# Last mixture of a gated four-layer block: sorted rows in a DRAM region for each expert, and another order of the stages

## The chip, the cores and the metric

The kernel runs on one core of a Trainium2 chip. Its time is the device time of one execution in microseconds (us). Engines are named as in the profile: PE (TensorE) with its weight loads PEld, DVE (VectorE), ACT (ScalarE), POOL (GpSimd) and SP (SyncE, which here only issues DMAs).

## The reference, cut to what matters

The input x holds 16 batches of 256 rows of 128 numbers. Four layers follow each other; each adds a gated cross attention (16 heads of 8 over 64 context rows) and then a gated feed-forward part:

```python
x = x + tanh(g_xattn[0]) * L0_xattn(layernorm(x), ctx, ctx)     # stage 0
x = x + tanh(g_ffn[0])   * L0_ffn(layernorm(x))                 # stage 1: mixture, best 2 of 8 experts, and a shared one
x = x + tanh(g_xattn[1]) * L1_xattn(layernorm(x), ctx, ctx, mask, side)  # stage 2
x = x + tanh(g_ffn[1])   * L1_ffn(layernorm(x))                 # stage 3: one ternary matrix
x = x + tanh(g_xattn[2]) * L2_xattn(...)                        # stage 4
x = x + tanh(g_ffn[2])   * L2_ffn(layernorm(x))                 # stage 5: one expert
x = x + tanh(g_xattn[3]) * L3_xattn(...)                        # stage 6
x = x + tanh(g_ffn[3])   * L3_ffn(layernorm(x))                 # stage 7: mixture, best 1 of 8 experts

def L3_ffn(t):                     # the part that is changed
    prob = softmax(t @ switch_w + switch_b)
    gate, e = max(prob), argmax(prob)          # first largest
    return gate * (gelu(t @ w1[e] + b1[e]) @ w2[e] + b2[e])      # 128 -> 512 -> 128
```

All is float32.

## The kernel before, in words

**Halves and blocks.** The batches are cut into two halves of 8 (hf 0 and 1). A half has 2048 rows, 16 row tiles of 128, and 4 blocks of 512 rows (two batches). x stays in SBUF (`xs`) through all layers. The halves depend on each other only through engines and buffers, so a stage of one half can run beside any stage of the other.

**The order is made by a planner in the kernel.** Each piece of work is a Python generator (`attention` for one batch, `queries`, `ffn_ternary`, `ffn_expert1`, `block`, `sorted_pair` and so on) that yields requests: `op(engine, length, needs)`, `dma(queue, size, needs)` or `get(slots, number, needs)`. `Order.run` (L173 to L201) takes the request that can begin first by its own assumed lengths, and of equal ones (rounded to 0.1 us) the one of the smallest rank; then the generator issues its instructions. So the program's order on PE, DVE, ACT and SP is that in which the planner took the requests, and POOL is chained to the same order (`chain_gpsimd`, L216). On the chip each engine runs its own instructions in that order and waits on semaphores; the planner's times play no part there. `RANKS` (L87) gives the rank of each of the 8 stages of each half, and `RATE` (L82) the assumed bytes per us of a DMA.

**A mixture (`mixture`, L1296, for l = 0 and l = 3).** For each block, `block` computes the layernorm, transposes it (`turned`), multiplies by the gate matrix (L1374) and puts the logits for 4 row tiles into a common tile `rt` (L1392). The normalized rows go to DRAM (`xrow`, L1345), and for l = 3 the rows of x beside them (L1351). When all four blocks of the half are done (`normed`), one chain on DVE does the routing for all 16 row tiles at once: softmax (L1410 to L1417), first largest (L1421 to L1428), counts by two matmuls (L1458, L1459), running sums (L1464), regions of the experts rounded up to 128 rows (L1471 to L1475), and then the inverse of the permutation: one-hot matrices (L1528, L1537, L1544) and 16 matmuls (L1549) give for each of n sorted rows the number of the row that belongs there. n = 16 k + 7 tiles: 39 for l = 0 (k = 2) and 23 for l = 3 (k = 1). The result is `index` (where a sorted row comes from), `place` (where its result goes) and, for l = 3, `gates`; `ex` holds the expert of each tile.

**The sorted tiles.** `fetch` (L1634) loads for each tile its expert's weights, 578 KB, by SP: the expert's number is read into a register (`value_load`, L1643), then the DMA is issued (L1647). There are 6 buffers `wb`. `sorted_pair` (L1652) works on two tiles: POOL gathers the rows by an indirect DMA (L1671, buffers `xg`), PE transposes them (L1684), DVE copies (L1688), PE does four matmuls a tile for the first matrix (L1698), ACT the gelu (L1705), PE four for the second (L1717), DVE adds the bias (L1727, after which `wb` is free) and, for l = 3, multiplies by the gate and adds x (L1734, after which `xg` is free); then POOL scatters the rows to the output (L1753). Between two indirect DMAs that would stand next to each other POOL gets a small addition (`apart`, L440). In float32 each matmul shows as two records. For l = 0 the results go to DRAM (`ysort`) and are gathered again (`collect`).

**Other lines that are named below.** Layernorm: L644, L645 (DVE), L647 to L650 (POOL), L656 (ACT). Attention ends with the projection L781 and the addition to x, L787. `make_fill1` loads the side input of layer 1's attention for one batch (four DMAs of 64 KB, three buffers) on SP, and POOL prepares it (L972).

Of the kernel before, what the change touches and what calls it, by code (L numbers as in the profile page):

```python
# [36 lines left out]
F32 = mybir.dt.float32  # L38
# [33 lines left out]


# [8 lines left out]
REACH, LAND, RATE, SWAP = 0.1, 1.8, 250e3, 1.3  # L82
# [4 lines left out]
RANKS = ((11, 14, 2, 14, 3, 5, 4, 14), (14, 14, 4, 14, 6, 9, 6, 2))  # L87
# [150 lines left out]
def flamingo_kernel(  # L238
# [91 lines left out]
    for l, k in ((0, 2), (3, 1)):  # L330
        n = sorted_tiles(k)
        for hf in range(2):
            wide = D if l == 0 else 2 * D
            xd = dram.tile([NT * P, wide], F32, name=f"xrow{l}{hf}", tag=f"xrow{l}{hf}")
            yd = None
            if l == 0:
                yd = dram.tile([n * P, D], F32, name=f"ysort{l}{hf}", tag=f"ysort{l}{hf}")
            srt[l, hf] = (k, n, xd, yd)
# [43 lines left out]
    starts = cst([1, nmax], "starts")  # L382

    id32 = cst([P, 32], "id32")
    ksel = cst([P, 2, 2, 2, 32], "ksel")
# [13 lines left out]
    label = cst([P, NT, 5], "label", BF16)  # L399
# [23 lines left out]
    big_s = slots("big", [P, 2, 512], 4)  # L423
    rc0_s = slots("rc0", [P, P], 3)
    wb_s = slots("wb", [P, NPK], 6)
    xg_s = slots("xg", [P, 2 * D], 6)
    xgT_s = slots("xgT", [P, 2 * P], 2)
    y_s = slots("y", [P, 2, D], 3)
# [6 lines left out]
    expert_s = slots("expert", [1, nmax], 2, I32)  # L435
# [53 lines left out]
    def constants():  # L489
# [31 lines left out]
        nc.vector.tensor_copy(label[:, :, 0:2], lab)  # L521
# [10 lines left out]
        nc.gpsimd.memset(carry[:, :, 0:1], 0.0)  # L532
        yield op(POOL, 0.5)
# [21 lines left out]
        nc.gpsimd.memset(ksel, 0.0)  # L555
        yield op(DVE, 0.5)
        for h in range(2):
            nc.vector.tensor_copy(
                ksel[:, h, :, h, :], id32.unsqueeze(1).to_broadcast([P, 2, 32])
            )  # L560
        yield op(DVE, 0.5)
        nc.vector.tensor_copy(id32b, id32)
        nc.vector.tensor_copy(kselb, ksel)
# [257 lines left out]
    def unit0(pair, t, rank):  # L821
# [57 lines left out]
        else:  # L879
            (sb,) = yield get(big_s, 1)  # L880
            sm = sb.ap.rearrange("p a b -> p (a b)")
# [108 lines left out]
    def attention(l, b, rank, end):  # L990
# [7 lines left out]
        i32, ks = (id32, ksel) if fb else (id32b, kselb)  # L998
# [226 lines left out]

    def add_four(blk, py, end, event, at):
# [30 lines left out]
    def ffn_expert1(blk, rank, begin, end):  # L1257

        (xn,) = yield get(xn_s, 1, begin[2 * blk], begin[2 * blk + 1])
        ats = yield from layernorm(blk, begin, xn.ap, xn)  # L1260
        (xf,) = yield get(xf_s, 1)
# [5 lines left out]
        (hb,) = yield get(big_s, 1)  # L1267
        h = hb.ap
# [24 lines left out]
    def bc8(a):  # L1293
        return a.unsqueeze(2).to_broadcast([P, NT, E])

    def mixture(l, hf, rank, begin, end):  # L1296

        k, n, xd, yd = srt[l, hf]
        b0 = HB * hf
        blks = range(NBLK // 2 * hf, NBLK // 2 * (hf + 1))  # L1300
        xnt = None
        if l == 0:
            (xnt,) = yield get(xnT_all_s, 1, begin[b0], moe_ready)
# [5 lines left out]

        index = st.ap[:, 4 * NT : 4 * NT + n].bitcast(I32)  # L1310
        place = st.ap[:, NT : NT + n].bitcast(I32)
        gates = st.ap[:, NT + n : NT + 2 * n]
# [17 lines left out]
        kept = Event(len(blks) * (1 if l == 0 else 3))  # L1330
# [18 lines left out]
        def keep_x(b):  # L1349
            at = yield dma(SP, 131e3, begin[b])  # L1350
            nc.sync.dma_start(rows(2 * (b - b0), 2)[:, :, D:], xs[b])  # L1351
            order.set(kept, at)

        def block(blk):
# [5 lines left out]
            if l == 3:  # L1360
                for b in (2 * blk, 2 * blk + 1):
                    order.task(rank, keep_x(b))
            xf = None
            if l == 0:
                dst, need = xnt.ap[:, blk - blks[0], :], xnt
            else:
                (xf,) = yield get(xf_s, 1)
                dst, need = xf.ap, xf
            pe, at = yield from turned(xn.ap, dst, ats, need)
# [3 lines left out]
            for t in range(4):  # L1373
# [3 lines left out]
                    gw0 if l == 0 else gw3,  # L1377
# [3 lines left out]
            if xf:  # L1381
                give(xf, xf_s, at)
            else:
                order.set(ev[blk], at)
# [3 lines left out]
            if l == 0:  # L1388
                nc.vector.tensor_copy(mine_, pl3)
            else:  # L1390
                swb = rows_sb[:, R_SWB : R_SWB + E]
                nc.vector.tensor_tensor(  # L1392
                    mine_, pl3, swb.unsqueeze(1).to_broadcast([P, 4, E]), ALU.add
                )
# [5 lines left out]
        if l == 0:  # L1400
            shared_left, routed = [len(blks)], Event()
            for blk in blks:
                order.task(rank + 0.6, shared_expert(blk, xnt, ev[blk], routed, end, rank, shared_left))
# [15 lines left out]
        def first_largest(p, m, oh):  # L1419

            nc.vector.tensor_reduce(m, p, AX.X, ALU.max)  # L1421
            nc.vector.tensor_tensor(oh, p, bc8(m), ALU.is_equal)

            nc.vector.scalar_tensor_tensor(
                oh, oh, 2.0 * E, falling.unsqueeze(1).to_broadcast([P, NT, E]), ALU.mult, ALU.add
            )
            nc.vector.tensor_reduce(c1, oh, AX.X, ALU.max)
            nc.vector.tensor_tensor(oh, oh, bc8(c1), ALU.is_equal)  # L1428

        yield op(DVE, 1.6)  # L1430
        first_largest(p3, m1, te(oh1))
        if k == 2:
            yield op(DVE, 1.9)
            nc.vector.scalar_tensor_tensor(te(p2), te(oh1), -2.0, p3, ALU.mult, ALU.add)
            first_largest(te(p2), m2, te(oh2))
            yield op(DVE, 0.6)
            nc.vector.tensor_tensor(den, m1, m2, ALU.add)
            nc.vector.reciprocal(den, den)
            for m in (m1, m2):
                nc.vector.tensor_tensor(m, m, den, ALU.mult)  # L1440
# [483 lines left out]
```

## Time and profile before

| | us |
|---|---|
| median of 3 runs | 1087.75 |
| lowest and highest | 1085.69, 1087.98 |
| the profiled execution | 1091.78 |
| its span in the profile | 1090.0 |

| engine | busy us | share of the span |
|---|---|---|
| PE | 914.4 | 84% |
| DVE | 670.9 | 62% |
| POOL | 644.8 | 59% |
| ACT | 575.9 | 53% |

The profile names groups of instructions by line, engine, operation and tiles (out<-in), with count, busy time, mean length, and the idle time of the engine before them with what ended it. The view by stretches gives for each stretch its length, the busy time of PE, PEld, DVE, ACT and POOL with the number of records, the granted clock of PE (1.00 is full), the share of time in which the DMA engines are busy, and GB/s. The timeline gives start, length, engine, line and operation. The weights are the largest traffic: 124 loads of 578.0 KB, of 114.36 MB in all. Half 1's last mixture is the end of the program: the last gate matmul (L1374) begins at 970.27 us, the routing's last DVE operation ends at 995.50, the last matmul (L1717) at 1083.26.

### The profile page before, as it was taken

Reading aid. Unit: us, or ns where it says so; the run is one execution under the profiler, and the core shown is the slowest. Engines: PE = TensorE matmul, PEld = TensorE weight load, DVE = VectorE, ACT = ScalarE, POOL = GpSimd, SP = SyncE. Lnnn points to the kernel's source line nnn. Section 1 sums busy time; section 2 is a strip of 40 time slices with the busy share of each in tenths; the row PEclk is TensorE's granted clock in tenths of the full one; section 3 lists DMA queues with packets and bytes.
Section 4 is the critical chain, followed back from the end, with each engine's and each line's share of the span. In section 5 each row is a group of like instructions: output and inputs, shape, how many; then the busy total and the mean of one; then the engine's idle time right before and its main releaser. Section 6 shows DMA issues by size and latency. Waiting matters only on the chain.

```text
span 1090.0 us, 27621 instructions
## 1 busy us (share of the span) xinstructions
PE 914.4 (84%) x10480; PEld 724.2 (66%) x10480; DVE 670.9 (62%) x1832; ACT 575.9 (53%) x1345; POOL 644.8 (59%) x1055
## 2 busy tenths in 40 slices
PE   5887568989788987789789899999998999777765
PEld 3776346878686886677556667667665667666664
DVE  4798897754464224366776767879789645446221
ACT  5454243656443454566446557765765667553332
POOL 5787636666834654765557656533444666744675
PEclk9899788979889998899999999999999999987987
DMA  6000004467764774633100100100000425544672
GB/s 195 2 12 21 23 1 147 132 211 237 231 153 162 227 228 141 228 93 112 52 17 20 29 16 21 36 21 7 24 9 2 161 59 156 189 145 144 215 259 60
DMA packets 63477, 114.36 MB, mean 105 GB/s; under 512 B 10289, under 2 KB 42552, under 8 KB 63344
## 3 DMA queue, kind: packets, MB, share of 16 engines
q1 hardware_dynamic: 54688, 94.22, 26.8%
q0 software_dynamic: 8224, 17.45, 6.0%
q8 instruction: 82, 1.34, 0.5%
q10 hardware_dynamic: 432, 0.93, 0.3%
q14 instruction: 51, 0.42, 0.1%
HBM read 99.06 MB, written 14.42 MB: 104 GB/s over the span
## 4 chain that ended last, share of the span: by engine, by line
PE 38%; DVE 12%; issue 8%; DMA 6%; POOL 5%; ACT 3%; another core or an unknown queue 2%; SPq 0%; POOLq 0%; DVEq 0%; ACTq 0%
PE bank L1698 6%; PE bank L1717 6%; DMA xg<-xrow,state 4%; DVE mx L1093 3%; PE bank L1008 3%; PE bank L1175 3%; PE bank L1072 2%; PE bank L781 2%; PE bank L1134 2%; PE bank L1014 2%; PE bank L747 1%; PE bank L1197 1%; PE bank L669 1%; PE bank L1621 1%
## 5 line engine op out<-in xcount | busy, mean ns | idle before, releaser
L1705 ACT ACTIVATE big<-bank,wb 128x128 f32<-128x128 f32 x496 | 138.5, 382 | 156.2 <-issue 98.6
L1698 PE MATMUL bank<-xgT,wb 128*128 128x128 f32 x992 | 147.5, 301 | 21.9 <-DVE xgT L1688 14.0
L1671 POOL DMA_INDIRECT xg<-xrow,state x124 | 121.9, 983 | 63.5 <-issue 27.9
L1698 PEld LDWEIGHTS bank<-xgT,wb 128*128 128x128 f32 x992 | 134.1, 212 | 31.7 <-DVE xgT L1688 18.6
L1717 PE MATMUL bank<-wb,big 128*128 128x128 f32 x992 | 133.6, 287 | 5.8 <-issue 4.8
L1717 PEld LDWEIGHTS bank<-wb,big 128*128 128x128 f32 x992 | 126.2, 200 | 13.8 <-issue 10.9
L656 ACT ACTIVATE xn<-x,ln 128x128 f32<-128x128 f32 x256 | 107.6, 494 | 52.5 <-POOL ln L650 52.2
L1727 DVE TENSOR_TENSOR y<-bank,wb 128x128 f32<-128x128 f32 x124 | 32.3, 285 | 115.4 <-PE bank L1717 90.9
L894 POOL TENSOR_TENSOR pT<-pT,rc 128x1024 f32<-128x1024 f32 x32 | 75.2, 2366 | 45.2 <-DVE rc L889 12.3
L1779 POOL DMA_INDIRECT yg<-ysort,state x64 | 62.9, 983 | 56.5 <-DVE x L1787 26.3
L1093 DVE TENSOR_REDUCE mx<-bank 128x8 f32<-128x512 f32 x128 | 81.4, 682 | 20.9 <-PE bank L1014 6.3
L1162 ACT ACTIVATE pT<-bank 128x512 f32<-128x512 f32 x128 | 67.2, 601 | 36.3 <-PE bank L1149 30.2
L677 POOL TENSOR_TENSOR x<-x,rows_sb 128x256 f32<-128x256 f32 x96 | 71.3, 761 | 12.5 <-ACT xn L656 11.8
L644 DVE BATCH_NORM_STATS2 ln<-x 128x6 f32<-128x128 f32 x256 | 68.6, 268 | 2.4 <-DMA x<-in_x_dram 2.2
L648 POOL TENSOR_TENSOR ln<-ln,mhalf 128x4 f32<-128x4 f32 x64 | 66.7, 1043 | 5.3
L1008 PE MATMUL bank<-kexp,qT 32*128 32x256 f32 x768 | 69.4, 413 | 0.2 <-DVE mx L1093 0.2
L647 POOL TENSOR_SCALAR ln<-ln 128x4 f32<-128x4 f32 x64 | 14.7, 230 | 90.9 <-DVE ln L645 83.7
L1753 POOL DMA_INDIRECT out_dram<-y,state x46 | 47.1, 1023 | 27.6 <-DVE y L1727 20.6
L1046 DVE TENSOR_REDUCE mx<-bank 128x8 f32<-128x512 f32 x64 | 43.5, 682 | 29.8 <-PE bank L1014 14.2
L1175 PE MATMUL bank<-pT,vx 128*32 128x256 f32 x768 | 60.3, 399 | 0.8 <-DVE pT L1054 0.5
L1688 DVE COPY xgT<-bank 128x256 f32<-128x256 f32 x64 | 25.9, 409 | 55.1 <-PE bank L1684 37.9
L1684 PE MATMUL bank<-ident,xg 128*128 128x128 f32 x124 | 29.4, 306 | 34.2 <-DMA xg<-xrow,state 30.1
(230 smaller groups left out, 2094.2 us busy)
## 6 DMA issues: line engine op xcount, KB each, us to landing
wb<-in_pk_l_dram SPq DMA_DIRECT2D x124, 578.0 KB
ysort<-y SPq DMA_DIRECT2D x38, 128.0 KB
xrow<-xn SPq DMA_DIRECT2D x16, 256.0 KB
fill<-in_fsideT_dram SPq DMA_DIRECT2D x64, 64.0 KB
x<-in_x_dram SPq DMA_DIRECT2D x16, 128.0 KB
xrow<-x SPq DMA_DIRECT2D x16, 128.0 KB
xg<-xrow,state POOLq DMA_INDIRECT x124
yg<-ysort,state POOLq DMA_INDIRECT x64
```

What stands on the lines that cost most here:

```text
L644: nc.vector.bn_stats(st[:, 2 * i + j, :], xs[b][:, j, :])
L656: nc.scalar.activation(xn[:, k, :], xs[b][:, j, :], AF.Identity, bias=nm[:, k : k + 1], scale=rs[:, k : k + 1],)
L677: nc.gpsimd.tensor_tensor(xs[b], xs[b], row.unsqueeze(1).to_broadcast([P, 2, D]), ALU.add)
L894: nc.gpsimd.tensor_tensor(s3, s3, rc.ap.unsqueeze(1).to_broadcast([P, 8, P]), ALU.mult)
L1008: nc.tensor.matmul(dst(g), qT[strip(g), ts], kexp[strip(g)].rearrange("p h k -> p (h k)"), start=True, stop=False,)
L1093: nc.vector.tensor_reduce(mx[:, :, g, :], sc[g].ap.rearrange("p (t h k) -> p t h k", h=4, k=S2), AX.X, ALU.max,)
L1162: nc.scalar.activation(pTs[g // 2].ap[:, (g % 2) * 512 : (g % 2 + 1) * 512], sc[g].ap, AF.Exp)
L1175: nc.tensor.matmul(po.ap[strip(g), i * S : (i + 1) * S], vx.ap[:, b % 2, c, :], pTs[c // 4].ap[:, (c % 4) * S : (c % 4 + 1) * S], start=Tr ...
L1671: nc.gpsimd.indirect_dma_start(out=xg[i], out_offset=None, in_=xd, in_offset=bass.IndirectOffsetOnAxis(ap=index[:, 2 * q + i : 2 * q + i + ...
L1698: nc.tensor.matmul(ph.ap[:, cs], wb[i].ap[:, cs], xgT.ap[:, i * P : (i + 1) * P], start=True, stop=True,)
L1705: nc.scalar.activation(hb.ap[:, i, cs], ph.ap[:, cs], func, bias=wb[i].ap[:, PK_B1 + c : PK_B1 + c + 1],)
L1717: nc.tensor.matmul(py.ap[:, i * D : (i + 1) * D], hb.ap[:, i, c * P : (c + 1) * P], wb[i].ap[:, PK_W2 + c * D : PK_W2 + (c + 1) * D], star ...
```

## The change

**The last mixture (l = 3) becomes a function of its own, `last_mixture`; the first one keeps the code above (`first_mixture`).** Each half gets a DRAM tensor of 17280 rows of 258 numbers: a region of 2048 rows for each of the 8 experts, and 7 x 128 rows to spare. A row holds the normalized row, the row of x, its number in the output and its gate. Each block does its own routing for 4 row tiles as soon as its logits are there: softmax, first largest, counts by two matmuls over 32 columns. `next_` holds for each expert the next free row of its region and runs on from block to block (a scan over 5 values an expert). POOL then scatters the block's 4 row tiles to their places in the regions (four indirect DMAs of 128 rows). ACT copies x beside the normalized rows in the tile that is scattered.

When all four blocks have counted, a short chain on DVE works out for each of the 23 tiles its expert and its first row in the regions (both to `ex`), and bounds that tell which of its rows are filled. A tile is now 128 rows that follow each other: SP reads the first row's number into a register and loads the tile by a plain DMA; POOL gathers nothing for l = 3. Gate and output row come with the rows; two small DVE operations a tile set the place of an unfilled row out of bounds. The scatter to the output is as before.

**The regions are filled once** with numbers (a piece of `rows_sb`), so that unfilled rows hold something finite: `fill_regions` issues 27 DMAs a half on SP, each of 128 x 5 rows; the planner is told to begin them at given stages.

**The planner** gets other ranks and RATE 280e3 for 250e3. Smaller edits: `ex` is given back by count (`done_with`), `big` is 1032 wide for 1024, `xg` 258 for 256, `y` 258 for 256 (the places are kept in it), the tile `ksel` is gone (it was only copied to `kselb`), `rt` is cut into four pieces after the second mixture of layer 0, and `ffn_expert1` takes its `big` buffer one step earlier.

```diff
-REACH, LAND, RATE, SWAP = 0.1, 1.8, 250e3, 1.3
+REACH, LAND, RATE, SWAP = 0.1, 1.8, 280e3, 1.3
-RANKS = ((11, 14, 2, 14, 3, 5, 4, 14), (14, 14, 4, 14, 6, 9, 6, 2))
+RANKS = ((10, 14, 14, 1, 1, 12, 8, 14), (14, 14, 2, 7, 5, 9, 10, 15))
...
+ROW3 = 2 * D + 2
+REGION = NT * P
+NROWS = E * REGION + (E - 1) * P
...
+    def last_mixture(hf, rank, begin):
...
+        next_ = st.ap[:, 4 * NT : 4 * NT + E]
+        yield op(DVE, 0.1, st)
+        nc.vector.tensor_copy(next_, region)
...
+        def block(blk):
...
+            (xn,) = yield get(big_s, 1, begin[bs[0]], begin[bs[1]])
+            rows = xn.ap.rearrange("p (t c) -> p t c", c=ROW3)
+            ats = yield from layernorm(blk, begin, rows[:, :, 0:D], xn)
...
+            for i, b in enumerate(bs):
+                yield op(ACT, 0.35, begin[b])
+                nc.scalar.copy(rows[:, 2 * i : 2 * i + 2, D : 2 * D], xs[b])
...
+            nc.tensor.matmul(pb.ap[:, 0:32], ones, cnt, start=True, stop=True)
+            nc.tensor.matmul(pb.ap[:, 32:64], before, cnt, start=True, stop=True)
...
+            nc.vector.tensor_tensor_scan(
+                upto, carry4.rearrange("p e t -> p (e t)"), acc, 0.0, ALU.mult, ALU.add
+            )
+            nc.vector.tensor_copy(next_, upto3[:, :, 4])
+            order.set(counted, at)
...
+            for t in range(t0, t0 + 4):
+                at = yield op(POOL, 1.3, placed)
+                part_indirect()
+                ins = nc.gpsimd.indirect_dma_start(
+                    out=xd,
+                    out_offset=bass.IndirectOffsetOnAxis(ap=pos[:, t : t + 1], axis=0),
+                    in_=rows[:, t - t0, :],
+                    in_offset=None,
+                )
+                unordered(ins, f"x{l}{hf}")
+                at = (at[0] + 2.2, "DMA")
+                order.set(kept, at)
...
+    def fill_regions(hf, whens):
+        xd = srt[3, hf][2].rearrange("(p a) c -> p a c", p=P)
+        n, m = NROWS // P, 5
+        for i in range(n // m):
+            yield dma(SP, 4.0 * P * m * ROW3, whens[i * m * len(whens) // n])
+            nc.sync.dma_start(
+                xd[:, m * i : m * (i + 1), :],
+                rows_sb[:, 0:ROW3].unsqueeze(1).to_broadcast([P, m, ROW3]),
+            )
...
         for i in range(m):
+            if l == 3:
+                yield op(SP, 0.4, *xgs, *needs)
+                r = nc.sync.value_load(
+                    ex.ap[0:1, n + 2 * q + i : n + 2 * q + i + 1], min_val=0, max_val=NROWS - P
+                )
+                at = yield dma(SP, 132e3)
+                nc.sync.dma_start(xg[i], xd[bass.ds(r, P), :])
+                done_with(ex, at)
+                continue
             at = yield op(POOL, 1.3, *xgs, *needs)
...
+                nc.vector.scalar_tensor_tensor(
+                    yi[i], yi[i], xg[i][:, 2 * D + 1 :], xg[i][:, D : 2 * D], ALU.mult, ALU.add
+                )
+                nc.vector.tensor_tensor(
+                    place[:, i : i + 1], xg[i][:, 2 * D : 2 * D + 1].bitcast(I32),
+                    filled[:, t : t + 1], ALU.bitwise_and,
+                )
+                nc.vector.tensor_tensor(
+                    place[:, i : i + 1], place[:, i : i + 1], empty[:, t : t + 1], ALU.bitwise_or
+                )
...
+    whens = [X[i][b] for i, h in ((5, 0), (6, 0), (3, 1), (4, 1)) for b in range(HB * h, HB * h + HB)]
+    for hf in range(2):
+        order.task(100.0, fill_regions(hf, whens[16 * hf : 16 * hf + 16]))
```

## The prediction

> **What bounds the kernel now.** I read the page's engine shares first, then TensorE's busy time in chosen stretches, then the groups of the last stretch, then the timeline of one pair of tiles there. The page says that TensorE (PE) leads, and the line by slices that it falls off at the end:
>
> ```profile
> PE 914.4 (84%) x10480; PEld 724.2 (66%) x10480; DVE 670.9 (62%) x1832; ACT 575.9 (53%) x1345; POOL 644.8 (59%) x1055
> PE   5887568989788987789789899999998999777765
> ```
>
> PE works 914 of 1090 us, so what a change of order can win is a part of the 176 us of idle. The stretches were cut where the work changes: 963.2 is the end of the last attention (the last addition on L787, at 963.23), 996 the end of half 1's routing, 1083.3 the last matmul.
>
> ```profile
> 480.00:890.00 410.00, 376.50 (x4693) 271.18 (x4693) 307.87 (x889) 249.63 (x544) 225.79 (x454) 0.98 0.14 40
> 890.00:963.20 73.20, 65.02 (x700) 51.39 (x700) 32.07 (x99) 49.33 (x114) 45.65 (x81) 0.95 0.46 143
> 963.20:996.00 32.80, 20.43 (x143) 18.36 (x141) 22.44 (x82) 11.82 (x33) 15.32 (x27) 0.80 0.45 138
> 996.00:1083.30 87.30, 62.49 (x439) 58.01 (x439) 19.91 (x64) 28.72 (x104) 58.19 (x96) 0.88 0.64 204
> ```
>
> The columns are length, busy PE, weight loads, DVE, ACT, POOL, then granted clock, DMA share and GB/s. The first two rows are idle 8% and 11%; the last two 38% and 28%, at a granted clock of 0.80 and 0.88. What PE waits for in the last one, by groups (busy, mean ns, then idle before and who ended it):
>
> ```profile
> L1698 PE MATMUL bank<-xgT,wb 128*128 128x128 f32 x208 | 32.9, 324 | 12.2 <-DVE xgT L1688 9.1 <-DVE y L1734 1.9 <-issue 1.1
> L1684 PE MATMUL bank<-ident,xg 128*128 128x128 f32 x23 | 6.2, 313 | 13.7 <-DMA xg<-xrow,state 13.7
> L1753 POOL DMA_INDIRECT out_dram<-y,state x25 | 25.4, 1015 | 17.2 <-DVE y L1727 14.5 <-issue 2.7
> L1671 POOL DMA_INDIRECT xg<-xrow,state x23 | 22.7, 986 | 18.5 <-issue 16.0 <-PE bank L1717 1.9 <-PE bank L1698 0.3
> ```
>
> Of the 24.8 us of idle, 13.7 are transposes that wait for gathered rows and 12.2 matmuls that wait for the copy of the transposes (the two overlap by a little). The gathers are late because POOL issues them in order among the scatters: 25 + 23 issues and 48 separators of 0.21 us fill 58 of 87 us. A stretch has 208/8 = 26 tiles, so a tile takes 87.3/26 = 3.36 us here, of which PE works 2.40. A pair whose rows are there looks like this:
>
> ```profile
> 1051.40 0.38 PE L1684 MATMUL bank<-ident,xg 128*128 128x128 f32 x2
> 1052.78 2.05 PE L1698 MATMUL bank<-xgT,wb 128*128 128x128 f32 x16
> 1054.66 2.12 PE L1717 MATMUL bank<-wb,big 128*128 128x128 f32 x16
> ```
>
> That is 0.38 + 2.05 + 2.12 = 4.55 us a pair, 2.28 a tile, and the next pair starts 5.2 us after (1056.62).
>
> **The change, part by part.** Both programs' orders of issue (they hold no times) give the tiles on each side of the last attention.
>
> *Moved: the last tiles.* Before the last attention there stood 15 first matmul groups (L1698), 12 second ones (L1717) and 16 transposes of half 0's tiles; in the changed program 6, 4 and 8. At 1.03, 1.04 and 0.19 us each (half of 2.05, and near half of 2.12 and 0.38) that is 9.3 + 8.3 + 1.5 = 19.1 us of PE work gone from in front of 963.2. With nothing else changed the last attention ends at 963.2 - 19.1 = 944.1.
>
> *Removed: the routing gap.* In 963.2 to 996 PE idles 12.4 us while the routing of all 16 row tiles runs on DVE (106 instructions for both halves, with one of 2.29 us and five of 0.49). It is replaced by a short chain for each block of 4: some 22 DVE operations at 0.16 to 0.30 us, about 5 us, an exponential, two small matmuls and four scatters at 1.02 + 0.36 us on POOL. Only the last block's chain follows the last attention: layernorm to gate took 963.57 to 971.23 (7.7 us), then 5 + 1.6 (table load 1.28 and 0.31) + 5.5 and a landing of up to 5, together 25 us. Behind the last attention stand 17 tiles of half 0 (40 first groups less half 1's 23), 17 x 2.7 = 46 us. So I cost it at nothing; if the tiles were gone it would cost its 25.
>
> *Replaced: the gathers.* 46 gathers leave POOL; 32 scatters of rows come, before the last stretch but for four to eight. POOL per tile falls from 2 x (1.0 + 0.21 + 0.15) = 2.7 us to 1.4. The rows now come by SP: one more register load and DMA for a tile. Weight loads that wait for nothing are issued about 1.17 us apart (the first two of the last stretch at 995.09 and 996.27), so SP takes 2.34 us a tile, just above PE's 2.28. The first row load of a half also waits for all 16 scatters of its half, and behind it stand the weights of the later pairs, as behind every waiting load all later weights and rows; for half 1 the 17 tiles above cover that, 46 us against 25. The ring: when a pair's buffers come free, SP needs 3 x 1.17 = 3.5 us to its fourth load; by the trace's DMA packets a weight load lands 3.2 to 6 us after its issue (the worst here 8.9); transposes, copy, matmuls and gelu to the addition take 6.7 (1046.39 to 1053.73, less some waiting). 3.5 + 5 + 6.7 = 15.2 us for three pairs is 2.5 us a tile, inside the next figure.
>
> *The pace of the last tiles.* Lower bound 2.28 (PE alone), upper bound 3.36 (nothing gained). I take 2.28 plus the wait for the copy, 12.2/26 = 0.47, and no wait for rows: 2.75. It is nearer the clean pair's 2.6. The trace gives the granted clock: 0.88 here, 1.00 between 650 and 750; the clean pair has the full rate. After the last attention stand 40 first groups, 42 second and 38 transposes, 41 tiles in round: 41 x 2.75 = 112.8 us; the last gate and counting matmuls 1.5; from the last matmul to the end 6.7 as now.
>
> [...]
>
> *Added: filling the regions.* 54 writes of 128 x 5 x 258 x 4 B = 660 KB, 35.7 MB, on SP after the first mixture. The nearest packets are those of 1024 B on SP's queue, 46 ns in the trace: 640 rows / 16 engines x 46 = 1.84 us each, 99 us in all. They stand between 480 and 850, where DMA is 4 to 32% busy. What else needs DMA there is half 1's side input (fill, 64 loads of 64 KB). Up to nine writes, 17 us, stand ahead of one such load; three buffers, each an attention of 10 us or more ahead, cover it. I take 0; with the cover gone, 18 writes ahead of those loads cost 33.
>
> *Small operations.* DVE: 310 added, 114 removed, some 62 against 25 us. The densest part, the second half of layer 3's attention, comes to 0.82 of PE's work; between 640 and 840 DVE had 164 against PE's 192, with PE 96% busy, so nothing on the path. ACT: 16 copies at 0.38 and two table loads at 1.28, 9 us, beside 576. PE: 32 one-hot matmuls less, 16 small ones more: nothing. SP: 24 stores less.
>
> *Other order of stages.* PE's work is the same; its idle time from 480 to 944 is now about 40 us (9%). At the quietest rate, that of 640 to 840 (4%), it would be 20 less; at that of 480 to 550 (57.95 of 70 busy, 17%) 40 more. I take 0, between the two, because the orders differ little up to half 0's first mixture, and later the same kinds of attention run beside each other.
>
> **The sum**: 944.1 + 112.8 + 1.5 + 6.7 = 1065.1 us of span; around the span lie 1091.78 - 1090.0 = 1.8, so 1066.9 against the profiled 1091.78. The median shown, 1087.75, is 0.9963 of that: 1063.
>
> **Rivals.**
> - *The end runs at PE's pace and the order is quieter too.* Speaks for it: the clean pairs, POOL at half its load. 41 x 0.47 = 19 us less gives 1044, with half of the quieter order 1034.
> - *The rows are late again*, now behind the weights on SP: 3.36 a tile, 25 us more, 1088: no change. For it: 2.34 us of issue a tile, a load landing after 8.9. Against: the ring above has slack. That the change doesn't do what it says ends here as well.
> - *Attention with nothing beside it.* Half 0's tiles filled the waits of layer 3's attention from 890 to 963; now they stand behind it, and 464 us run as 480 to 550 did: 40 us more, 1103, slower. It decides from 25 us, an idle share of 14% instead of 9%. Against it: 640 to 840 has two attentions side by side at 4%.
>
> **The numbers.** Forecast 1063 (1048 to 1078) 0.50; first rival 0.17; second (1078 to 1091) 0.17, of which 0.11 are faster, 0.05 within 0.2% and 0.01 slower; third 0.16. Faster 0.78, same 0.05, slower 0.17 (0.2%, about 2 us, is what a measurement can tell). The range 1036 to 1092 leaves out some 0.05 below and 0.15 above.
>
> **What would show it.** The last attention ends near 944, and no stretch behind it has the 38% of idle; the last tiles stand 2.75 us apart, transposes wait little for rows, POOL is half idle there, the clock above 0.88. Wrong if transposes wait for rows from SP over 0.3 us a tile, if the stretch from 480 to the last attention idles more than 14%, or if POOL waits for the side input.

## The result, and the profile after

On the chip of the prediction's profile, the first chip below, the changed kernel took 1074.59 us (median of 9 runs, 1070.26 to 1082.18) against 1089.31 of the kernel before (9 runs, 1085.69 to 1098.28): a ratio of 0.985, 95% interval 0.983 to 0.988. The forecast was 1063 in 1036 to 1092, so it held the time and the sign there, 12 us too low. On two other chips the sign did not hold: the kernel before took about 1038 us on each (medians 1038.19 and 1037.59), and the changed one was 1.013 (1.006 to 1.019) and 1.009 (1.005 to 1.012) of it. Both results have to be explained. Ratios and their intervals leave out a run that lies over 1.5% above the fastest of its kernel; medians keep it.

The profiled execution of the changed kernel took 1074.29 us with a span of 1072.6. First the page, its engine shares and PE's row by slices:

```profile
PE 908.7 (85%) x10472; PEld 722.2 (67%) x10472; DVE 689.9 (64%) x2027; ACT 585.3 (55%) x1369; POOL 633.8 (59%) x1032
PE   5888578989879787989987999999999987977875
```

PE's work is nearly the same (914.4 before); the last slices are fuller. The view by stretches, cut at the last attention's end (939.4) and the last matmul's (1064.1):

```profile
480.00:890.00 410.00, 379.60 (x4724) 274.05 (x4726) 299.31 (x914) 255.97 (x558) 228.46 (x457) 0.97 0.47 113
890.00:939.40 49.40, 42.43 (x478) 32.71 (x471) 31.33 (x125) 30.14 (x74) 25.93 (x50) 0.90 0.52 174
939.40:1000.00 60.60, 46.83 (x331) 45.03 (x330) 31.86 (x155) 27.47 (x83) 35.75 (x60) 0.85 0.73 234
1000.00:1064.10 64.10, 51.49 (x386) 49.42 (x385) 21.58 (x96) 25.74 (x92) 25.96 (x42) 0.90 0.75 243
```

The stretch with 38% of idle is gone: behind the last attention PE now idles 23% and then 20%. But that end is longer than forecast. These are the groups of 939.4 to 1064.1 that PE and POOL wait in:

```profile
L1881 PE MATMUL bank<-xgT,wb 128*128 128x128 f32 x320 | 51.1, 321 | 19.0 <-DVE y L1927 13.0 <-DVE xgT L1871 4.7 <-issue 1.4
L1867 PE MATMUL bank<-ident,xg 128*128 128x128 f32 x38 | 8.5, 288 | 2.2 <-DMA xg<-xrow 2.2
L1653 PE MATMUL bank<-rt,ones 128*128 128x32 f32 x4 | 0.8, 286 | 5.1 <-DVE rt L1649 3.0 <-DVE rt L1332 2.1
L1947 POOL DMA_INDIRECT out_dram<-y x39 | 39.4, 1010 | 53.9 <-DVE y L1912 50.8 <-issue 2.5 <-DVE rt L1642 0.2
```

(L1881 is before's L1698, the first matmuls of a tile; L1867 was L1684, the transposes; L1902 was L1717, the second matmuls; L1912 was L1727, the addition; L1871 was L1688, the copy.) Rows are no longer late: the transposes' wait fell from 13.7 us to 2.2. POOL now waits for results instead of being waited for. The new name is `DVE y L1927`, the second place operation of a tile: 13.0 us of PE's waits stand under it. But of DVE's work these matmuls read only `xgT`, the copy, which comes just behind that operation on DVE. In two other profiles of this kernel the same wait stands under the copy's own name (14.1 and 14.4 us). So both names are one wait, 17.7 us here. The timeline of one pair shows what is late:

```profile
1047.66 2.08 PE L1902 MATMUL bank<-wb,big 128*128 128x128 f32 x16
...
1049.57 0.38 PE L1867 MATMUL bank<-ident,xg 128*128 128x128 f32 x2
...
1050.23 0.29 DVE L1912 TENSOR_TENSOR y<-bank,wb 128x128 f32<-128x128 f32 x1 [2.18 <-PE bank L1867]
1050.55 0.35 DVE L1919 SCALAR_TENSOR_TENSOR y<-y,xg 128x128 f32<-128x128 f32 x1
1050.82 0.15 DVE L1923 TENSOR_TENSOR y<-xg,state 128x1 int32<-128x1 int32 x1
1051.01 0.16 DVE L1927 TENSOR_TENSOR y<-y,state 128x1 int32<-128x1 int32 x1
...
1051.95 0.42 DVE L1871 COPY xgT<-bank 128x256 f32<-128x256 f32 x1
...
1052.43 2.55 PE L1881 MATMUL bank<-xgT,wb 128*128 128x128 f32 x16 [2.48 <-DVE y L1927]
```

PE ends a pair's second matmuls and the next pair's transposes at 1049.95 and then stands for 2.48 us. PE goes on 0.06 us after the copy's end. DVE has eight operations of the pair before (two tiles, four each) in front of the copy, and the first of them starts only at 1050.23, behind the second tile's matmuls, since both tiles share a bank.

### The profile page after: what moved, and what is told of

Read it like the earlier page. It is cut to its first block, busy times and chain, and to the rows that moved or that the text cites. A ratio compares the mean times of both kernels' runs of the same rounds, so it can differ in the third digit from the quotient of the medians.

```text
span 1072.6 us, 28097 instructions
## 1 busy us (share of the span) xinstructions
PE 908.7 (85%) x10472; PEld 722.2 (67%) x10472; DVE 689.9 (64%) x2027; ACT 585.3 (55%) x1369; POOL 633.8 (59%) x1032
## 4 chain that ended last, share of the span: by engine, by line
PE 36%; DVE 15%; DMA 6%; issue 5%; POOL 5%; ACT 3%; SPq 1%; another core or an unknown queue 1%; POOLq 0%; DVEq 0%; ACTq 0%
PE bank L1881 6%; PE bank L1902 5%; PE bank L1033 4%; PE bank L1200 3%; DVE mx L1118 3%; DMA xg<-xrow,state 3%; PE bank L1159 2%; PE bank L1097 2%; PE bank L1222 2%; PE bank L1039 2%; PE bank L806 1%; DVE ln L669 1%; DVE mx L1071 1%; PE bank L694 1%; PE bank L1867 1%
## 5 line engine op out<-in xcount | busy, mean ns | idle before, releaser
L1881 PE MATMUL bank<-xgT,wb 128*128 128x128 f32 x992 | 146.4, 301 | 28.8 <-DVE y L1927 13.0
L1881 PEld LDWEIGHTS bank<-xgT,wb 128*128 128x128 f32 x992 | 132.8, 211 | 40.5 <-DVE y L1927 14.4
L1902 PE MATMUL bank<-wb,big 128*128 128x128 f32 x992 | 131.5, 285 | 0.6 <-ACT big L1888 0.5
L1902 PEld LDWEIGHTS bank<-wb,big 128*128 128x128 f32 x992 | 124.3, 200 | 3.5 <-issue 1.7
L681 ACT ACTIVATE xn<-x,ln 128x128 f32<-128x128 f32 x224 | 94.5, 496 | 50.6 <-POOL ln L675 50.1
L1118 DVE TENSOR_REDUCE mx<-bank 128x8 f32<-128x512 f32 x128 | 81.2, 682 | 15.9 <-PE bank L1039 7.9
L1912 DVE TENSOR_TENSOR y<-bank,wb 128x128 f32<-128x128 f32 x124 | 32.4, 287 | 87.1 <-PE bank L1902 74.5
L1853 POOL DMA_INDIRECT xg<-xrow,state x78 | 76.8, 985 | 13.7 <-issue 6.0
L1947 POOL DMA_INDIRECT out_dram<-y x46 | 46.6, 1012 | 62.9 <-DVE y L1912 57.3
L1187 ACT ACTIVATE pT<-bank 128x512 f32<-128x512 f32 x128 | 67.1, 602 | 21.4 <-PE bank L1174 20.8
L1033 PE MATMUL bank<-kexp,qT 32*128 32x256 f32 x768 | 72.8, 428 | 6.3 <-DVE pT L1079 5.5
L672 POOL TENSOR_SCALAR ln<-ln 128x4 f32<-128x4 f32 x64 | 14.8, 232 | 104.7 <-DVE ln L670 95.9
L1871 DVE COPY xgT<-bank 128x256 f32<-128x256 f32 x64 | 26.4, 414 | 66.1 <-PE bank L1867 52.8
L1103 ACT ACTIVATE pT<-bank 128x512 f32<-128x512 f32 x64 | 37.4, 599 | 36.5 <-PE bank L1097 33.1
L670 DVE BATCH_NORM_AGGREGATE ln<-ln 128x2 f32<-128x6 f32 x256 | 46.6, 182 | 10.2
```

The costliest lines, as they stand in the source:

```text
L681: nc.scalar.activation(xn[:, k, :], xs[b][:, j, :], AF.Identity, bias=nm[:, k : k + 1], scale=rs[:, k : k + 1],)
L1033: nc.tensor.matmul(dst(g), qT[strip(g), ts], kexp[strip(g)].rearrange("p h k -> p (h k)"), start=True, stop=False,)
L1118: nc.vector.tensor_reduce(mx[:, :, g, :], sc[g].ap.rearrange("p (t h k) -> p t h k", h=4, k=S2), AX.X, ALU.max,)
L1187: nc.scalar.activation(pTs[g // 2].ap[:, (g % 2) * 512 : (g % 2 + 1) * 512], sc[g].ap, AF.Exp)
L1853: nc.gpsimd.indirect_dma_start(out=xg[i], out_offset=None, in_=xd, in_offset=bass.IndirectOffsetOnAxis(ap=index[:, 2 * q + i : 2 * q + i + ...
L1881: nc.tensor.matmul(ph.ap[:, cs], wb[i].ap[:, cs], xgT.ap[:, i * P : (i + 1) * P], start=True, stop=True,)
```

## The experiments

One measure serves for all: the tail, from the last attention's last projection to the last matmul, with PE's busy time in it by PE's records. It depends on the chip less than the whole time does: 119.2 and 120.1 us for the kernel before. For the changed one there are four profiles of an unedited tail, three of the kernel itself and one in which only the fills ahead of it are doubled: 117.8 to 124.7 us, of which PE idles 21.9 to 26.4. Each row is one profiled execution, so only what lies outside these bounds can be put down to an edit. The busy time differs too, with the granted clock of the tail in the last column; a wait that an edit removes must show in the idle time.

| kernel | tail us | PE busy | PE idle | clock |
|---|---|---|---|---|
| before, first profile | 120.1 | 82.9 | 37.2 | 0.86 |
| changed, first profile | 124.7 | 98.3 | 26.4 | 0.88 |
| copy on ACT | 122.1 | 94.0 | 28.1 | 0.93 |
| place operations early | 121.4 | 95.6 | 25.8 | 0.91 |
| two banks | 115.3 | 92.1 | 23.2 | 0.93 |
| copy first | 123.0 | 95.8 | 27.2 | 0.93 |
| changed, chip of the next part | 120.4 | 97.4 | 23.0 | 0.89 |
| before, chip of the last runs | 119.2 | 85.2 | 34.0 | 0.84 |
| changed, same chip | 121.1 | 97.4 | 23.7 | 0.89 |
| changed with the fills twice, same chip | 117.8 | 95.9 | 21.9 | 0.90 |
| two banks and early, same chip | 108.0 | 91.8 | 16.2 | 0.92 |

### What sets the pace of the tail

Four kernels, each the changed one with one edit. They ran on a chip where the kernel before took 1099.85 us. The changed kernel did not run there, so their whole times can't be held against its own; the four ratios to the kernel before, 0.979 to 0.987, have intervals that overlap each other and the 0.983 to 0.988 of the changed kernel on the first chip.

**Copy on ACT.**

```diff
-        nc.vector.tensor_copy(xgT.ap[:, 0 : m * P], pt.ap[:, 0 : m * P])
+        if l == 3:
+            nc.scalar.copy(xgT.ap[:, 0 : m * P], pt.ap[:, 0 : m * P])
+        else:
+            nc.vector.tensor_copy(xgT.ap[:, 0 : m * P], pt.ap[:, 0 : m * P])
```

> Change: in the last mixture the copy of the transposes out of the bank (xgT) runs on ACT instead of DVE; order of issue on PE, DVE and SP unchanged. Theory A (the tail's pace is set by the order on DVE: the copy stands behind both tiles' additions and place operations of the pair before; 17.7 us of PE's waits between 939 and 1064 are for it): the waits for DVE go and a bare copy of about 0.5 us is left, 10 to 14 us less, so 1061 to 1065 us. Theory B (the pace is set by SP's issue and the ring of three pairs of weight buffers; the copy only looks late): the same idle time comes back as waits for rows or weights, 1071 to 1077. If ACT's gelus (0.38 us each, eight a pair) stand ahead of the copy instead, the waits stay with ACT's name.

Measured: 1082.17 us, 0.983 (0.978 to 0.987) of before; the tail 122.1. The 17.7 us of waits for DVE went, and came back under two other names. PE's waits in its tail (us in total, times, longest):

```profile
PE bank L1867 <- DMA xg<-xrow: 10.5, 9, 4.6
PE bank L1884 <- ACT xgT L1872: 9.4, 10, 2.5
```

So theory A in this form falls: with the copy taken out from behind the additions PE idles 28.1 us, not 10 to 14 less than in the unedited tails. The additions were not moved: SP's weight loads still wait 15.8 us for them (21.0 in the changed kernel's first profile), since an addition releases a weight buffer. That the rows are late because they stand behind those loads on SP is argued, not shown.

**Place operations early.** The two operations on `place` move from behind the addition to behind the copy, into `places[q % 4 + 4 * hf]`, eight new tiles of two columns.

> Change: the two place operations of each last tile (about 0.17 us each) are issued just after the pair's copy, with a buffer of their own, instead of behind the tile's addition. Theory A: the chain in front of the next pair's copy gets 4 x 0.17 = 0.7 us shorter at each of the 5 to 8 places where PE waits for it: 3.5 to 5.5 us less, 1069 to 1071. Theory B: no change, 1073 to 1076.

Measured: 1086.23 us, 0.987 (0.981 to 0.993); tail 121.4. Both the tail and its 25.8 us of idle time lie within those of the unedited tails, so no gain is shown, and neither theory is told from the other.

**Two banks.**

```diff
-        (py,) = yield get(banks, 1)
+        pys = yield get(banks, m if l == 3 else 1)
+        ats = []
         for i in range(m):
+            py = pys[i % len(pys)]
             at = yield op(PE, 0.9, hts[i], py)
+            ats.append(at)
...
-            yt = yield op(DVE, 0.25 if l == 0 else 0.75, at, y)
+            py = pys[i % len(pys)]
+            yt = yield op(DVE, 0.25 if l == 0 else 0.75, ats[i] if l == 3 else at, y)
```

> Change: in the last mixture each tile of a pair has a bank of its own for its second matmuls, so that the first tile's addition needn't wait for the second tile's matmuls. Theory A: the first addition with its three followers (0.86 us) moves out from in front of the next pair's copy, at 5 to 8 places: 4 to 7 us less, 1067 to 1070. Theory B: no change, 1073 to 1076. One bank more is held in each pair; if banks are short there, it is slower.

Measured: 1082.82 us, 0.979 (0.972 to 0.987); tail 115.3, 2.5 us under the shortest unedited one. But PE's idle time in it, 23.2 us, is not shorter, and its waits for the copy are 17.3 us (14.2, and 1.9 and 1.2 under the names of operations before it). What is shorter is the busy time, at a clock of 0.93 and with the first matmuls of one tile less behind the last attention (39 tiles for 40). So the edit does free the first tile's addition from the second tile's matmuls, but that it brings the copy sooner by itself is not shown.

**Copy first.** `op(...)` gets a field that lowers the rank of the copy by 0.0015 where two requests can begin at the same time.

> Change: where the planner finds the copy of the next pair and an addition of the pair before able to start at the same time, the copy goes first (last mixture only). Theory A: one addition with its followers (0.86 us) leaves the path at 5 to 8 places, 4 to 7 us less, 1067 to 1070; the additions it delays free the weight buffers 0.4 us later, which costs nothing if the ring has slack. Theory B: buffers come free later and SP's loads with them, 1074 to 1078.

Measured: 1085.4 us, 0.986 (0.982 to 0.991); tail 123.0. The gain of 4 to 7 us did not come. PE idles 27.2 us, and waits 18.2 for the copy (13.5 under its own name, 4.7 under that of the place operation) against 14.1 to 17.7 in the unedited tails. The first addition still stands behind the second tile's matmuls there; that this is why nothing was gained is argued.

**Rows issued by ACT, with two banks.** `nc.sync.value_load` and `nc.sync.dma_start` of the row loads become those of `nc.scalar`. It ran on a chip where the kernel before took 1038.19 us, as did the three runs of the next part.

> Change: two banks for the second matmuls of a pair as in the run before, and the row loads of the last mixture issued by ACT instead of SP (register load and DMA both). In the two-bank run SP issued a load every 1.2 us without a break from 1026 to 1063, 4.8 us a pair. Theory B2 (with the DVE order mended, SP's issue is the next limit): SP falls to 2.4 us a pair, the tail goes to 2.6 to 2.7 us a tile, 7 to 10 us less than with two banks alone: 0.970 to 0.974 of before. Theory A2 (SP only looks busy because buffers come free at that pace; the chain rows, transposes, copy, gelu sets it): 0.977 to 0.981 as with two banks alone. If a row load that waits for its buffer holds up ACT's gelus behind it: 0.985 or more.

Measured: 1072.03 us, 1.033 (1.026 to 1.039) of before, 20 us over the changed kernel beside it. The planner put 45 first groups behind the last attention instead of 40, and a tile took 3.05 us. Its SP waited 101.2 us for additions, so SP was free; PE waited 13.0 us for rows and 13.1 for the copy. A row load on ACT stands in order among gelus. Relieving SP in this way costs more than it gives, and doesn't tell whether SP was the limit.

**Two banks and place operations early**, both edits together:

> Change: two banks for a pair's second matmuls, and the place operations just behind the pair's copy, both as in the single runs. Theory A (order on DVE): both savings add up to 6 to 10 us under the changed kernel beside it, the tail at 2.75 us a tile. Theory B (SP's issue of 1.17 us a load): no better than two banks alone, 3 to 7 us under the changed kernel, the tail at 2.85.

Measured: 1034.95 us, 0.997 (0.994 to 1.000) of before on a chip where the changed kernel took 1047.68: 12.7 us under it, more than either theory expected. The tail accounts for it, 108.0 us for 41 tiles or 2.63 each, 9.8 us under the shortest unedited one. It is the best version found: 1.2% better than the changed kernel, and on that chip level with the kernel before. Of the 13.0 us between the two tails on this chip 7.5 are idle time. These are PE's waits in the changed kernel's tail there, and then with both edits:

```profile
PE bank L1881 <- DVE xgT L1871: 14.4, 9, 3.9
PE bank L1867 <- DMA xg<-xrow: 5.1, 6, 3.8
```

```profile
PE bank L1868 <- DMA xg<-xrow: 9.3, 7, 4.5
PE bank L1893 <- DVE xgT L1872: 6.1, 9, 0.9
```

The waits for the copy fell from 14.4 us to 6.1, the longest from 3.9 to 0.9. The other 5.6 us are busy time: one tile's first matmuls less, as with two banks alone, and a clock of 0.92 for 0.89; whether the shorter waits bring the higher clock is open. SP has little time left now. These are its loads in that tail (a row joins two of a kind):

```profile
1006.32 1.51 SPq L1823 DMA_DIRECT2D wb<-in_pk_l_dram  x2
1008.62 1.50 SPq L1849 DMA_DIRECT2D xg<-xrow  x2
...
1015.53 1.48 SPq L1823 DMA_DIRECT2D wb<-in_pk_l_dram  x2
```

From 1006.32 to 1015.53 two pairs are 9.2 us, four loads every 4.6 us without a break, 2.3 us a tile: the prediction's 2.34 of issue. But this is not what PE's 9.3 us for rows come from. From 1000 us on it waits 0.3 us for rows. The two long waits, 7.8 us, stand together at the first rows of half 1 (966 to 976 us):

```profile
PE bank L1868 <- DMA xg<-xrow: 7.8, 2, 4.5
SPq L1849 <- DMA xrow<-big,state: 3.6, 1, 3.6
```

There SP itself waits, for the last scatters into the regions. So theory A is shown for the two edits together, not for each; theory B's sign, no better than two banks alone, did not come, and that SP's issue is the next limit is not shown.

### What the two halves of the change are worth alone

> The changed kernel once more, as a measure for the runs beside it, since this chip may be slower than the first by about a per cent. All theories: 0.985 of the kernel before, 125 to 127 us from the last attention's projection to the last matmul.

Measured: 1052.28 us, and 1.013 (1.006 to 1.019) of before; tail 120.4. Neither came as expected: the tail was shorter than 125 to 127, and the ratio has the other sign.

**The new mixture in the old order** (`RANKS` and `RATE` of the kernel before):

> Change: the new last mixture with the ranks and the wire rate of the kernel before. If the gain is the mixture's and the order of stages is worth nothing (the prediction's 0): 0.983 to 0.988 of before. If the order gives the gain: 0.995 to 1.005. If the new mixture needs the new order (rows of half 1 late, weights of later pairs behind them): above 1.00.

Measured: 1078.15 us, 1.037 (1.029 to 1.045). Third case: the new mixture needs the new order. In its tail PE idles 42.7 of 114.8 us (23.0 of 120.4 in the changed kernel beside it), most of it for rows of the regions, once for long:

```profile
PE bank L1867 <- DMA xg<-xrow: 28.4, 5, 17.8
```

Only 28 tiles stood behind the last attention there, and half 1's rows, which wait for the last block's routing and scatters, were not covered.

**The old mixture in the new order** (`RANKS` and `RATE` of the changed kernel):

> Change: the kernel before with the ranks and the wire rate of the changed one; the last mixture stays as it was, with the routing of a half in one piece and gathers on POOL. If the order is worth nothing by itself: 0.998 to 1.005 of before. If the order gives the gain: 0.985 to 0.99. If this order leaves the one-piece routing with less work beside it: 1.01 to 1.03.

Measured: 1088.87 us, 1.048 (1.041 to 1.054), beyond the third case. The last attention ends 6 us sooner than in the kernel before (908.4 against 914.6 in the run of the kernel before on the last chip, which has the same time), but the tail takes 177.8 us. PE's waits in it:

```profile
PE bank L1684 <- DMA xg<-xrow,state: 34.8, 13, 6.8
PE bank L1698 <- DVE xgT L1688: 11.2, 12, 1.5
PE bank L1549 <- DVE big L1544: 10.6, 1, 10.6
```

The gathers through POOL and the routing in one piece are what this order can't hide. On that chip the mixture costs 40 us alone and the order 51 us alone, together 14. In the new order the mixture saves 36.6 us (1088.87 to 1052.28); with the new mixture the order saves 25.9. They can't be priced one by one and added.

### What the fills of the regions cost

```diff
             nc.sync.dma_start(
                 xd[:, m * i : m * (i + 1), :],
                 rows_sb[:, 0:ROW3].unsqueeze(1).to_broadcast([P, m, ROW3]),
             )
+            nc.sync.dma_start(
+                spare[hf].rearrange("(p a) c -> p a c", p=P)[:, m * i : m * (i + 1), :],
+                rows_sb[:, 0:ROW3].unsqueeze(1).to_broadcast([P, m, ROW3]),
+            )
```

> Change: each of the 54 writes that fill the regions is issued twice, the second to spare regions that nothing reads: 35.7 MB more, and 54 more issues on SP. If the fills are hidden, as the prediction costs them at 0: within 3 us of the changed kernel. If what stands behind them on SP's queue (side input, stores, weights) waits for them: 10 to 33 us more, with POOL's wait for the side input grown from 14 us.

Measured: 1107.23 us, 1.067 (1.061 to 1.072) of before, 59.6 over the changed kernel on the same chip. The size is beyond the second case, and the place is another. POOL and PE in the timeline:

```profile
857.77 1.13 POOL L1681 DMA_INDIRECT xrow<-big,state  x1 [44.04 <-issue]
```

```profile
865.71 0.39 PE L1141 MATMUL bank<-identb,mx 128*128 128x128 bf16 x2 [42.24 <-POOL mx L1132]
```

L1681 is the first scatter of rows. It stands 44.04 us in POOL's order, and behind it stand POOL's steps on an attention's mask (up to L1132), which PE waits for. The view names no releaser, but the trace has the times of the semaphores: POOL's wait ends at 856.85 us, and one of those that it waits for, which the fills raise as they land, was raised last at 856.83. SP issues fills until 861, and rows may not be scattered into a region before it is filled. This one wait of PE is 42 of the 57 us by which the last attention ends later (977.6 for 920.7). It is not the side input, for which POOL waits 10.9 us here and 18.4 in the changed kernel on this chip. In the changed kernel the last fill's packets end at 768 us and the first scatter is issued at 810, so the fills are hidden with some 42 us to spare, and the prediction's 0 was right for one dose. Its price was not: back to back the fills were issued 3.0 us apart (24 from 687 to 756), not 1.84.

### Why the sign depends on the chip

> The kernel before once more, with a profile. On one chip it took 1089 us and the changed one 0.985 of it, on another 1038 us and the changed one 1.013 of it. Theory C (the kernel before lives on waits for gathered rows and results through DMA, so a chip whose transfers land sooner, or whose clock is granted higher, helps it more than the changed one): where this chip is a quick one (before under 1060), the routing gap behind the last attention and the transposes' waits for gathers are shorter than the 12.4 and 13.7 us of the first profile, and its clock is above 0.935; where it is a slow one, about 1085 to 1100 us with the same stages as first. Rival: only the stages ahead of 480 us differ between chips, then the two kernels' lasts stand as in the first profiles.

> The changed kernel on the same chip as the run of the kernel before beside it. On a slow chip 0.985 of before, on a quick one 1.01. Its tail from the last attention to the last matmul 120 to 125 us either way.

Measured: the kernel before 1038.59 us, the changed one 1047.68, 1.009 (1.005 to 1.012). Stretches of the kernel before, first on the first chip, then on this one, cut at the same instructions:

```profile
354.00:640.00 286.00, 244.96 (x2528) 193.48 (x2527) 159.18 (x451) 156.68 (x377) 178.55 (x311) 0.95 0.36 110
640.00:963.20 323.20, 303.02 (x3784) 221.38 (x3783) 229.00 (x673) 206.44 (x450) 167.60 (x345) 0.98 0.19 59
963.20:1083.30 120.10, 82.91 (x582) 76.37 (x580) 42.35 (x144) 40.53 (x137) 73.51 (x122) 0.86 0.59 186
```

```profile
349.00:603.00 254.00, 233.90 (x2530) 187.25 (x2530) 158.88 (x451) 157.13 (x378) 179.01 (x311) 0.98 0.40 124
603.00:914.60 311.60, 297.04 (x3781) 219.18 (x3781) 228.27 (x673) 206.04 (x449) 168.90 (x346) 0.99 0.20 61
914.60:1033.80 119.20, 85.24 (x583) 79.58 (x581) 42.51 (x144) 40.70 (x137) 73.70 (x122) 0.84 0.59 188
```

Of the 49 us, 5 lie ahead of these rows, 32 in the first, 12 in the second, and 1 in the tail. In the first row PE's idle falls from 41.0 us to 20.1, and its busy time from 245.0 to 233.9. Theory C's mechanism falls: the tail with its late gathers is the same on both chips, though the clock is above 0.935 as it said (0.940). Its rival is nearer, but "ahead of 480" was too narrow. What differs can be seen by name. PE and DVE of the kernel before on the first chip, the largest:

```profile
PE bank L1717 <- issue: 4.8, 3, 2.6
...
DVE mx L1046 <- remote: 11.0, 2, 9.0
DVE y L1727 <- remote: 6.6, 1, 6.6
```

On this chip the whole list of this kind for PE is

```profile
PE bank L1698 <- issue: 0.7, 1, 0.7
```

"Issue" and "remote" stand for idle time for which the profile shows no releaser. Over the whole execution PE has 18.1 us of it on the first chip and 0.7 here, DVE 25.0 and 1.4. The changed kernel has 18.8 on PE and 6.1 on DVE on the first chip, none and 1.0 here. So both kernels lose time on the first chip to stops that neither shows here. They are not the whole difference. In the profiled executions the kernel before is 49.4 us shorter here, of which 23.4 are PE's busy time (914.4 to 891.1, at a mean clock of 0.927 and 0.940) and 26.0 idle time; the changed one is 22.3 us shorter, 13.6 busy and 8.7 idle. What stops the engines, and why the kernel before gains twice as much, is open. The runs of each chip of the experiments were taken in one session, so they can't tell the chip from the session.

## Why the prediction was right and wrong, step by step

- **The last attention ends at 944.1.** On the first chip 939.4, 4.7 sooner; PE's busy time ahead of it fell by 21.0 us (831.4 to 810.4), near the 19.1. On the chip of the last runs 920.7 against the kernel before's 914.6, where the step would have said 895.5, 25 us less. "I take 0" for the other order of stages is the step that failed there: PE's idle time ahead of the last attention is 14.1 us more. The rest is busy time, only 8.0 us less instead of 19.1, though as many groups moved as on the first chip; the clock up to there is 0.939 against 0.952. Part of the idle time is in the first mixture, whose transposes wait longer in the new order (changed kernel from 354 to 480 us, then kernel before from 349 to 480, same chip):

```profile
PE bank L1867 <- DMA xg<-xrow,state: 12.6, 9, 2.7
```

```profile
PE bank L1684 <- DMA xg<-xrow,state: 4.6, 5, 2.5
```

- **The routing gap at nothing.** Right in the new order, and the condition named was the right one: with the cover gone, in the old order, one wait for rows took 17.8 us (the step said 25). Four small counting matmuls still wait 5.1 us for DVE.
- **41 tiles at 2.75 us, and 1.5.** The tail took 124.7 us instead of 114.3; this is the term that was mis-sized (120.4 and 121.1 on the other two chips). Without the 1.5 it is 3.0 us a tile: PE's work is 2.36 and not 2.28, at a granted clock of 0.85 to 0.90 in the tail and 1.00 in the clean pair; and the idle time is 26.4 us instead of 41 x 0.47 = 19.3.
- **No wait for rows.** Right: 2.2 us (5.2 and 5.1 on the other chips). The second rival's 3.36 a tile would have made the tail 25 us longer than forecast. By the order of the trace's packets, an estimate, the 36 weight loads of the tail landed 4.6 us after their issue on average (3.0 to 6.5) and the 36 row loads behind them 3.6 (2.1 to 5.0). A row load landed at about the time of the weight load issued before it (1.8 us sooner to 2.9 later), and PE's wait for rows was still only the 2.2 us.
- **Small operations, "nothing on the path".** Not borne out in the tail. DVE's share there is 43%, yet in the pair shown eight operations stand in front of the copy, four of them the added place operations. The share of a stretch says nothing about what stands in front of one instruction. What the place operations cost by themselves is not shown.
- **SP at 2.34 us a tile.** Right as a pace of issue: 2.3 with both DVE edits made. That it is the next limit is not shown.
- **The fills at 0.** Right, with 42 us to spare. POOL's wait for the side input, named as a sign of being wrong, grew from 9.3 to 14.0 us on the first chip, but nothing in its trace waits for what POOL makes of it. What waits first when the cover is gone is a scatter on POOL, not the side input, and 33 for it was too low.
- **The end, 6.7 us.** 8.5 (1064.1 to 1072.6), on all three chips.
- **The rivals.** The third gave the sign of the two quicker chips, but not by its mechanism: from 480 to the last attention PE idles 8% on the first chip and 6% on the other, both under its 14%. The second didn't come about, nor the first. The point "clock above 0.88" is borderline: 0.88 for the tail, 0.89 on the other two chips.

In sum on the first chip: 4.7 sooner, 10.4 later, 1.8 later give 7.5 us over the forecast span of 1065.1. So the time on the first chip is in part luck: two steps that erred in opposite directions. The sign rested on the profile of one chip. On the chip of the last runs the kernel before has 26 us less of idle time and the changed one only 9, and the moved tiles save less busy time.

## What to carry to other kernels

Price an order of stages and the piece of work that it is to cover together; the idle time that one leaves is the cover of the other: here each alone cost 40 and 51 us, both together 14. When a wait goes, look at the instruction order of the engine behind it, one pair of tiles at a time: here the additions of a pair waited for a bank shared by two tiles and the next copy stood behind them, and two short edits together gave back 12.7 us, where no single one shortened PE's idle time clear of the scatter. Where a gain is about 1%, measure on more than one chip before you believe its sign.

## What the runs showed of the hardware

- The same program differed by 6% between chips, or their sessions (1038 to 1100 us for the kernel before), and two programs differed unequally (the changed kernel was 0.985, 1.013 and 1.009 of before); the tail from the last attention on differed less (119 and 120 us). Stops of PE and DVE without a releaser, up to 9.0 us each, appeared on the slower chips alone; on the quicker ones none was over 0.74.
- A load by a register on SP took 1.12 to 1.18 us in the kernel before when nothing held it: in SP's records the register load is 0.27 us, the arithmetic behind it 0.15, the DMA's issue 0.33, the rest small steps and gaps.
- With the DMA engines full (685 to 756 us of the changed kernel, a busy share of 1.05) the fills and what ran beside them moved 17.22 MB in 71 us, 243 GB/s, in packets of 1032 bytes for the most part; the 1024-byte packets of the profile before, at a median of 46 ns, had suggested 360, an estimate with 16 engines. Issued back to back a fill took 3.0 us, not the 1.84 of the prediction.
